# Layer 1 of a four-layer image network: the deformable convolution gathers centered depthwise channels first and multiplies afterwards

## The chip, the cores and the metric

The kernel runs on one core of a Trainium2 chip. A core has five engines that work side by side: TensorE (PE) multiplies matrices, VectorE (DVE) and ScalarE (ACT) work on tiles of 128 partitions, GpSimd (POOL) and SyncE (SP) here mostly start transfers. Sixteen DMA engines move data between the chip's DRAM and the on-chip memory (SBUF). Matrix products land in PSUM, which has eight banks of 128 partitions by 512 f32 values. The metric is the device time of one execution in microseconds (us); lower is better. All arithmetic is f32.

## The reference

The network has four layers on 2 images of 512 channels and 32 x 32 pixels (1024 pixels). Layer 0 is an attention with sampled keys and an MLP, layer 2 a linear attention, layer 3 a normal attention with 8 heads. The change is in layer 1:

```python
x1 = x[:, :256]
x2 = x[:, 256:]
d = conv3x3_depthwise(x1, dw_w, dw_b)          # 256 channels
d = conv1x1(d, pw_w, pw_b)                     # 256 -> 512 channels
mu = d.mean(axis=(2, 3)); var = d.var(axis=(2, 3))
d = (d - mu) / sqrt(var + EPS)                 # per image and channel
off = conv3x3(d, off_w, off_b)                 # 512 -> 18 = 9 taps x (dy, dx)
samples = sum over 4 corners of d[corner] * weight[corner]   # per tap and pixel
dc = einsum('bckhw,ock->bohw', samples, dc_w) + dc_b         # 9 taps, 512 -> 512
dc = layernorm_over_channels(dc) * ln_g + ln_b
das = d * sigmoid(dc)
g = sigmoid(dsc2(max of x2) + dsc2(mean of x2))
x = x * das + x * g
```

A corner outside the image counts as zero. Each tap of each pixel has its own position, read from `off`, so the four corners are gathered by an index.

## The kernel before

The two images are worked one after the other. TensorE's instructions are in an order written by hand: the phases are Python generators, each `yield` is a place where another phase may put its own instructions, and `layers()` (L275) pulls the generators in turn with the helpers `some` and `weave`. The order of the other engines follows from a planner that knows what depends on what. So, if an instruction on TensorE waits, all that stands behind it on TensorE waits too. Memory is given out from pools that open and close like a stack on a left and a right side; a tile that takes memory which another pool has left waits until the last access to it is over.

Layer 1 of image 0 lies beside the MLP of image 1 (`mlp.run(1)`, 32 steps of 8 matmuls). `FOUND` (L449) says how many steps of the features are taken at each MLP step, and from step `MADE` (L450) on two steps of products are taken at each. The phases of layer 1:

- `Features.features` (L1084 on): the depthwise convolution on VectorE (nine operations of 128x1024 for each half of the channels, L1125 and L1129), the channel gate g, the pointwise matmuls (L1145), statistics on VectorE, and the normalised d (L1163).
- `Features.offsets`: d is copied into a tile with a border of zeros, the offset convolution takes 9 taps x 4 channel groups x 4 strips of pixels = 144 matmul instructions for each image (L1186), VectorE adds the bias, and `samples` (L1244) turns positions into indices and the weights of the four corners.
- `Products` (L1293): products first, samples afterwards. For each tap k, d times the tap's 512x512 weights is made for all pixels, in 8 chunks of 128 pixels with 4 matmuls each (L1324). ScalarE copies each result (L1332) and SP writes it to a table in DRAM (L1333), one table of 1024 x 512 for each image and tap. The tap's 1 MB of weights is loaded one tap ahead into one of two buffers.
- `Samples` (L1340): for each tap and chunk two indirect DMAs by POOL (L1376), one for each row of corners, fetch two neighbouring pixels of 512 channels for each of 128 partitions, 512 KB each. VectorE multiplies each corner by its weight and adds it to `dfacc` (L1387): 4 operations of 128x512 for each tap and chunk. `due` lets a tap's gathers begin when its table is whole.
- `gate_image` (L1397): layernorm of `dfacc`, transposes back to channels by pixels, sigmoid, and the new x.

`Linear` (L1450) is layer 2, `Attention` (L1652) layer 3. Its query and key weights `w_q`, `w_k` are loaded at L380, early in the stretch; its weights for the values come later. The products of image 1 are woven with the last samples of image 0, the gate of image 0 and layer 2 of image 0. The queries and keys of layer 3 for image 0 lie beside the last samples of image 1, the values beside layer 2 of image 1 (`BESIDE`, L454). Layer 3 proper starts behind that.

The loop in which the samples are weighed, and the product:

```python
for s in range(4):
    self.net.nc.vector.scalar_tensor_tensor(
        acc, g[:, s, :], self.f.wts[:, c, k, s : s + 1],
        self.f.bias if (k, s) == (0, 0) else acc, ALU.mult, ALU.add)
```

Of the kernel before, what the change touches and what calls it, by code (L numbers as in the profile page):

```python
# [106 lines left out]
def layouts(i):  # L107
# [43 lines left out]
    for h in range(2):  # L151
# [21 lines left out]
        "pw_w": _rows(np.asarray(i["L1_conv_pw_w"]).reshape(C, 256).T),  # L173
        "a_pw_w": _rows(np.asarray(i["L1_conv_a_pw_w"]).reshape(C, 256).T),
# [100 lines left out]
def layers(net, out):  # L275
# [12 lines left out]
    with ExitStack() as later:  # L288
# [41 lines left out]
        with room, ExitStack() as l0b:  # L330
# [20 lines left out]
            products = Products(net, image0, dram, side="right")  # L351
            own0 = ExitStack()
            f0 = Features(net, 0, own0, side="right")
            with ExitStack() as ctx:
                banks["turn"] = net.psum(ctx, "ft_ps", 2), "turn"
                found = f0.run(turn, False)
                made = products.run(f0, turn)
                taken = None
                for i, _ in enumerate(mlp.run(1)):
                    some(found, FOUND[i] if i < len(FOUND) else 0)  # L360
                    if i == len(FOUND):
                        some(found, 99)
                        sums0 = Samples(net, f0, products, own0, 3, side="right")
                        taken = sums0.run()
                    if i >= MADE:
                        for _ in range(2):
                            next(made)

                            if taken is not None and i < 30:
                                sums0.due(taken)  # L370
        with ExitStack() as l1:

            ps_m = net.psum(l1, "l1_m", 5)
            kv_bank = net.bank(l1, "l2_kv")
            banks["turn"] = net.psum(l1, "l1_y", 2), "turn"

            def bank(name):
                return ps_m.tile([128, 512], F32, name=name, tag="bank")

            att = Attention(net, later)  # L380
            l2 = ExitStack()
            linear = Linear(net, l2)
            own1 = ExitStack()
            f1 = Features(net, 1, own1)
            more = net.pool(own1, "df_more", 1)
            sums0.pools += [more]
            found = f1.run(bank, True)
            for i, _ in enumerate(made):
                if i > 1:
                    some(found, 2)  # L390
                if i % 4 < 3:
                    sums0.due(taken)
            some(found, 99)
            sums1 = Samples(net, f1, products, own1, 1)
            sums1.pools += [more]
            tmp = net.pool(own1, "df_tmp", 1)
            made = products.run(f1, turn)
            taken1 = sums1.run()
            aside, ctx2 = None, None
            for i, _ in enumerate(made):  # L400
                if aside is None:
                    if next(taken, None) is None:
                        aside = gate_image(net, f0, sums0, tmp, bank)
                        wait = i + 4
                    continue
                sums1.due(taken1)
                if ctx2 is None and i >= wait:
                    if next(aside) != "gated" and next(aside) != "gated":
                        continue
                    own0.close()  # L410
                    ctx2 = ExitStack()
                    linear.open(ctx2, side="right")
                    extra = net.pool(own1, "df_extra", 4)
                    sums1.pools += [extra] * 4
                    aside = chain(
                        linear.run(0, bank, kv_bank),
                        group_norm_terms(net, linear.tmp, 0, bank),
                    )
                elif ctx2 is not None and i % 3 < 2:
                    next(aside, None)  # L420
            for _ in aside:
                next(taken1, None)
            ctx2.close()
            image0.close()

            att.open_first(later, side="right")
            for _ in att.normalize(0):
                next(taken1, None)
            keys = chain(*(att.queries_keys(0, hp, turn) for hp in range(CC)))
            for i in range(48):  # L430
                next(keys)
                if i % 2 == 0:
                    next(taken1, None)
            some(taken1, 99)
            weave(keys, gate_image(net, f1, sums1, tmp, bank))
            own1.close()
            with ExitStack() as ctx:
                att.open_values(later, side="right")
                linear.open(ctx)
                values = att.values(0, turn)  # L440
                for i, _ in enumerate(linear.run(1, bank, kv_bank)):
                    some(values, BESIDE[i])
            l2.close()
# [5 lines left out]
FOUND = (1, 0, 0, 1, 2, 2, 2, 2, 0, 1, 1, 0, 3, 3, 3)  # L449
MADE = 11  # L450
# [633 lines left out]
class Features:  # L1084
# [4 lines left out]
    def __init__(self, net, b, ctx, **kw):  # L1089
# [4 lines left out]
        self.idx = small.tile([128, 2, 8, 9], mybir.dt.int32, name="idx", tag="idx")  # L1094
        self.wts = small.tile([128, 8, 9, 4], F32, name="wts", tag="wts")
        self.bias = net.load_row("dc_b_row", small)

    def run(self, bank, spread):


        with ExitStack() as ctx:
            yield from self.features(ctx, bank, spread)
        with ExitStack() as ctx:
            yield from self.offsets(ctx, bank, spread)

    def features(self, ctx, bank, spread):
# [3 lines left out]
        self.pw_w, self.a_pw_w = net.load("pw_w", w), net.load("a_pw_w", w)  # L1110
        x_pad = w.tile([128, 34, 34], F32, name="x_pad", tag="x_pad")
        nc.gpsimd.memset(x_pad, 0.0)  # L1112


        dw = tmp.tile([128, 2, 32, 32], F32, name="dw", tag="dw")
        for cc in range(2):
            nc.scalar.copy(
                x_pad[:, 1:33, 1:33], x[:, b, cc, :].rearrange("p (y x) -> p y x", x=32)
            )
            acc = dw[:, cc, :, :]  # L1120
            for t in range(9):
                ky, kx = divmod(t, 3)
                view = x_pad[:, ky : ky + 32, kx : kx + 32]
# [10 lines left out]
        yield  # L1134
        self.channel_gate(bank)
# [3 lines left out]
        flat = dw.rearrange("p c y x -> p c (y x)")  # L1139
        for oc in range(CC):  # L1140
# [15 lines left out]
            mv = tmp.tile([128, 2], F32, name="mv", tag="mv", bufs=2)  # L1156
            nc.vector.bn_aggr(mv, stats)
            rstd = tmp.tile([128, 1], F32, name="rstd", tag="rstd", bufs=2)
            nc.vector.tensor_scalar(rstd, mv[:, 1:2], 1e-5, None, ALU.add)
            nc.scalar.activation(rstd, rstd, AF.Sqrt)  # L1160
            nc.vector.reciprocal(rstd, rstd)
            part = d[:, oc, :]
            nc.vector.tensor_scalar(part, part, mv[:, 0:1], rstd, ALU.subtract, ALU.mult)  # L1163
        yield

    def offsets(self, ctx, bank, spread):
# [4 lines left out]
        d_pad = w.tile([128, CC, 34, 34], F32, name="d_pad", tag="d_pad")  # L1171
        nc.gpsimd.memset(d_pad, 0.0)
        for cc in range(CC):
            nc.scalar.copy(
                d_pad[:, cc, 1:33, 1:33], self.d[:, cc, :].rearrange("p (y x) -> p y x", x=32)
            )
        for _ in range(9 if spread else 1):
            yield


        po = bank("po")
        for t in range(9):
            ky, kx = divmod(t, 3)
            for cc in range(CC):
                for n in range(4):
                    nc.tensor.matmul(  # L1186
                        po[32 * n : 32 * n + 18, :256].rearrange("p (y x) -> p y x", x=32),
                        lhsT=self.off_w[:, cc, t, :],
                        rhs=d_pad[:, cc, 8 * n + ky : 8 * n + ky + 8, kx : kx + 32],
                        start=(t == 0 and cc == 0),  # L1190
                        stop=(t == 8 and cc == CC - 1),
                        skip_group_check=True,
                    )
            yield
# [7 lines left out]
        self.samples(pos, bank)  # L1202

# [40 lines left out]
    def samples(self, pos, bank):  # L1244
# [11 lines left out]
        def new(name, dtype=F32, tag=None):  # L1256
# [14 lines left out]
        row = tmp.tile([128, 8, 9], F32, name="row", tag="row")  # L1271
        nc.vector.scalar_tensor_tensor(
            row, first[:, :, :, 0], 32.0, first[:, :, :, 1], ALU.mult, ALU.add
        )
        for dy in range(2):
            nc.vector.tensor_scalar(self.idx[:, dy], row, 32.0 * dy, None, ALU.add)
# [9 lines left out]
        for k in range(4):  # L1286
            dy, dx = divmod(k, 2)
            nc.vector.tensor_tensor(
                wts[:, :, :, k], near[dy][:, :, :, 0], near[dx][:, :, :, 1], ALU.mult
            )  # L1290


class Products:  # L1293
# [4 lines left out]
    def __init__(self, net, ctx, dram, **kw):  # L1298
        self.net = net
        self.wt = net.pool(ctx, "df_w", 2, **kw)  # L1300
        self.out = net.pool(ctx, "df_y", 4, **kw)
        self.tables = {}
        for b in range(B):
            for k in range(9):
                self.tables[b, k] = dram.tile([HW, C], F32, name="table", tag=f"table{b}_{k}")
        self.made = {(b, k): 0 for b in range(B) for k in range(9)}

    def weights(self, k):
        t = self.wt.tile([128, CC, C], F32, name="dc_w_t", tag="dc_w")
# [669 lines left out]
```

## Time and profile before

| | us |
|---|---|
| median of 3 runs (3950.36 to 3961.6) | 3961.13 |
| the profiled execution, its time | 3949.34 |
| its span, first to last instruction | 3947.6 |
| MLP of image 1 begins | 2420.9 |
| first logits of layer 3 (L1803) | 3406.6 |

The profile is that of one execution. A row of a group of instructions has the line in the program, the engine, the operation, output and inputs, the shape, the count; then busy time in us and the mean of one in ns; then the idle time of the engine ahead of these instructions, and what ended it. In the row of a DMA the last number is the median time in us from issue to landing. A row of a stretch has its length, then for each engine its busy time and the number of its records, the granted clock of TensorE as a share of full speed, the share of the time in which a DMA engine was busy, and GB/s. The rows of the largest groups in the rest of the program are, for comparison:

```profile
L835 PE MATMUL ph<-h,w_t 128*32 128x512 f32 x16384 | 1799.0, 593 | 14.0 <-ACT lo L845 6.4
L1059 PE MATMUL ph<-xn,room 128*128 128x512 f32 x512 | 229.6, 592 | 0.0
L1855 PE MATMUL pt<-cst_t,e 128*128 128x128 f32 x1024 | 148.9, 278 | 6.3 <-ACT aT L1866 3.6
```

### The profile page before, as it was taken

The page shows a single profiled execution, that of the slowest core. Times are in us where ns is not written, and L with a number is a line of the kernel's source. Part 1 is how long each engine was busy: PE and PEld are TensorE (multiplying, and loading weights), DVE is VectorE, ACT ScalarE, POOL GpSimd, SP SyncE. Part 2 cuts the span into 40 slices and gives each one's busy share as a digit, 9 for nine tenths or more (in the row PEclk, how much of TensorE's full clock was granted, in tenths as well). Part 3 has the DMA queues.
Part 4 walks back from the last instruction along what each step waited for, and adds up shares of the span by engine and source line. Part 5 has one row for each costly group of instructions (what it writes and reads, how often), then busy time and mean ns, then how long its engine had stood idle before and what let it go on. Part 6 is the DMA issues. An engine that isn't in the chain of part 4 may idle for free.

```text
span 3947.6 us, 60251 instructions
## 1 busy us (share of the span) xinstructions
PE 3837.4 (97%) x25580; PEld 1516.4 (38%) x25580; DVE 2951.5 (75%) x3312; ACT 2539.7 (64%) x2866; POOL 347.9 (9%) x324
## 2 busy tenths in 40 slices
PE   7999999999999999999998999999898999999999
PEld 4432232222322222222333444444343444455555
DVE  6999999999999999999995114043576887566565
ACT  7999999999999999999994211211121212245544
POOL 0000000000000000000000000032363553000000
PEclk9999999999999999999998999999999999999999
DMA  3000000000000000000011000065677996000000
GB/s 108 1 23 22 23 23 1 22 23 23 12 12 23 23 22 1 23 23 22 1 54 54 0 0 24 21 209 194 254 284 274 346 357 224 1 5 8 1 19 25
DMA packets 90482, 274.82 MB, mean 70 GB/s; under 512 B 9141, under 2 KB 10677, under 8 KB 86885
## 3 DMA queue, kind: packets, MB, share of 16 engines
q0 software_dynamic: 42432, 154.39, 10.7%
q1 hardware_dynamic: 47780, 116.58, 8.2%
q8 instruction: 202, 3.31, 0.3%
q14 instruction: 68, 0.55, 0.0%
HBM read 228.72 MB, written 42.21 MB: 69 GB/s over the span
## 4 chain that ended last, share of the span: by engine, by line
PE 76%; ACT 10%; DVE 6%; DMA 4%; issue 2%; POOL 1%; SPq 0%; POOLq 0%; ACTq 0%; DVEq 0%
PE ph L835 36%; PE py L1324 6%; PE ph L1059 5%; PE acc L1048 5%; PE sim L856 4%; ACT h L824 3%; PE pl L1803 3%; DVE dfacc L1387 3%; DMA got<-table,idx 3%; PE pq L1736 3%; PE po L1818 3%; PE pt L1855 3%; ACT hi L847 2%; ACT lo L845 2%; ACT ab L480 2%
## 5 line engine op out<-in xcount | busy, mean ns | idle before, releaser
L835 PE MATMUL ph<-h,w_t 128*32 128x512 f32 x16384 | 1799.0, 593 | 14.0 <-ACT lo L845 6.4
L815 DVE TENSOR_TENSOR h<-ab 128x1024 f32<-128x1024 f32 x1024 | 1205.4, 1218 | 74.6 <-PE ph L835 73.5
L835 PEld LDWEIGHTS ph<-h,w_t 128*32 128x32 f32 x16384 | 547.5, 110 | 1238.2 <-issue 1066.3
L824 ACT ACTIVATE h<-h 128x1024 f32<-128x1024 f32 x832 | 870.4, 1066 | 41.3 <-DVE h L815 40.4
L848 DVE SCALAR_TENSOR_TENSOR hi<-lo,low_w,hi 128x1024 f32<-128x1024 f32 x512 | 654.4, 1278 | 27.6 <-ACT hi L847 27.0
L847 ACT ACTIVATE hi<-ph,size_b,size 128x1024 f32<-128x1024 f32 x512 | 620.4, 1212 | 16.3 <-PE ph L835 10.5
L845 ACT ACTIVATE lo<-ph,vec_t 128x1024 f32<-128x1024 f32 x512 | 571.1, 1115 | 5.0 <-PE ph L835 5.0
L1387 DVE SCALAR_TENSOR_TENSOR dfacc<-got,wts,dfacc 128x512 f32<-128x512 f32 x560 | 402.3, 746 | 197.9 <-DMA got<-table,idx 190.4
L1324 PE MATMUL py<-dc_w_t,d 128*128 128x512 f32 x1152 | 519.4, 606 | 24.8 <-ACT y L1332 24.8
L1332 ACT COPY y<-py 128x512 f32<-128x512 f32 x144 | 83.3, 584 | 474.1 <-PE py L1324 442.1
L1376 POOL DMA_INDIRECT got<-table,idx x288 | 328.0, 1139 | 459.1 <-DVE dfacc L1387 152.4
L1324 PEld LDWEIGHTS py<-dc_w_t,d 128*128 128x128 f32 x1152 | 220.1, 194 | 303.0 <-issue 266.6
L1901 ACT ACTIVATE e<-pl,m 128x1024 f32<-128x1024 f32 x128 | 143.5, 1121 | 224.5 <-DVE m L1893 224.5
L1893 DVE TENSOR_REDUCE m<-pl 128x1 f32<-128x1024 f32 x128 | 150.7, 1219 | 145.0 <-PE pl L1803 145.0
L856 PE MATMUL sim<-hi,w 128*32 128x512 f32 x2048 | 246.8, 592 | 0.6 <-DVE hi L848 0.6
L1059 PE MATMUL ph<-xn,room 128*128 128x512 f32 x512 | 229.6, 592 | 0.0
L1048 PE MATMUL acc<-h,mlp_w_t 128*128 128x512 f32 x512 | 229.2, 592 | 0.0
L1067 ACT ACTIVATE h<-ph,vec_t 128x512 f32<-128x512 f32 x64 | 44.0, 687 | 247.6 <-PE ph L1059 247.5
L1112 POOL MEMSET x_pad<- 128x1156 f32 x2 | 2.1, 1068 | 2086.8 <-PE pb L959 2086.8
L1855 PE MATMUL pt<-cst_t,e 128*128 128x128 f32 x1024 | 148.9, 278 | 6.3 <-ACT aT L1866 3.6
L1855 PEld LDWEIGHTS pt<-cst_t,e 128*128 128x128 f32 x1024 | 118.6, 142 | 93.7 <-issue 61.7
L1048 PEld LDWEIGHTS acc<-h,mlp_w_t 128*128 128x128 f32 x512 | 97.3, 190 | 122.4 <-issue 122.4
(232 smaller groups left out, 2457.1 us busy)
## 6 DMA issues: line engine op xcount, KB each, us to landing
table<-y SPq DMA_DIRECT2D x144, 256.0 KB, 5.6
ab<-feat_d SPq DMA_DIRECT2D x64, 512.0 KB, 4.3
dc_w_t<-in_dc_w_dram SPq DMA_DIRECT2D x18, 1024.0 KB, 6.1
got<-table,idx POOLq DMA_INDIRECT x288, 7.0
room<-in_mlp_w_dram SPq DMA_DIRECT2D x1, 4096.0 KB, 15.6
mlp_w_t<-in_mlp_w_dram SPq DMA_DIRECT2D x1, 4096.0 KB, 12.0
w_qkv_t<-in_w_qkv_dram SPq DMA_DIRECT2D x3, 1024.0 KB, 5.3
out_dram<-x_all SPq DMA_DIRECT2D x12, 256.0 KB, 2.0
```

Of the source, the lines that this page charges most:

```text
L815: nc.vector.tensor_tensor(h1.rearrange("p (y x) -> p y x", x=32), at_x[:, k : k + 1, :].to_broadcast([128, 32, 32]), at_y[:, k, :].unsquee ...
L824: nc.scalar.activation(h1, h1, AF.Relu)
L835: nc.tensor.matmul(ph[32 * t : 32 * t + 32, half(n)], lhsT=w2[:, c0 : c0 + 32], rhs=pair[t // 2][:, half(n)], start=True, stop=True, skip_ ...
L845: nc.scalar.activation(lo, phs[0], AF.Relu, bias=b2_lo)
L847: nc.scalar.activation(hi, phs[1], AF.Relu, bias=size_b, scale=size)
L848: nc.vector.scalar_tensor_tensor(hi, lo, low_w, hi, ALU.mult, ALU.add)
L856: nc.tensor.matmul(sim[32 * t : 32 * t + 32, half(n)], lhsT=w3[:, 30 - j : 62 - j], rhs=sums[t][:, half(n)], start=(j == 0), stop=(j == 30 ...
L1048: nc.tensor.matmul(accs[oc], lhsT=self.w2[:, m, 128 * oc : 128 * oc + 128], rhs=hs[m], start=(m == 0), stop=(m == 15),)
L1059: nc.tensor.matmul(ph, lhsT=self.w1[:, k, 128 * m : 128 * m + 128], rhs=xn[:, k, :], start=(k == 0), stop=(k == CC - 1),)
L1324: nc.tensor.matmul(py, lhsT=f.d[:, cc, 128 * c : 128 * c + 128], rhs=w[:, cc, :], start=(cc == 0), stop=(cc == CC - 1),)
L1387: self.net.nc.vector.scalar_tensor_tensor(acc, g[:, s, :], self.f.wts[:, c, k, s : s + 1], self.f.bias if (k, s) == (0, 0) else acc, ALU.mult,
L1855: nc.tensor.transpose(pt[:, 128 * c : 128 * c + 128], e[:, 128 * k : 128 * k + 128], ident)
```

## The change

Samples and products change places. The pointwise convolution is linear, and its output is normalised per channel, so d is the pointwise weights, scaled by 1/std, times the depthwise channels less their mean over the image; the biases drop out. The sum over corners can then be made on the 256 depthwise channels, and the pointwise weights can be multiplied into the weights of the offset and of the deformable convolution beforehand.

- The depthwise output is centered on VectorE and copied into the bordered tile `pad`. d itself is still made by the pointwise matmuls, for the gate; its normalisation and the channel gate move to the end of `offsets`.
- TensorE transposes the centered channels (16 transposes for each image), and four DMAs by SP write one table for each image: 1024 pixels x (the pixel, the pixel one row below) x 256 channels, 2 MB. One gather of two neighbouring pixels brings all four corners, 512 KB: 72 gathers for each image instead of 144.
- The offset weights are folded with the scaled pointwise weights `pw_n` (8 matmuls of 162 columns), and the offset convolution has 72 instructions for each image instead of 144. The offset weights' tile is now in a pool that opens when the pools of `features` have closed.
- `Folded`: for each tap and half of the channels 4 matmuls make the folded weights, 72 matmuls for each image. Image 0 loads each tap's weights into the tile `out_w` of layer 0, one buffer; image 1 has two.
- `Deform`: VectorE sums the corners of two samples (a pair; 36 pairs for each image), TensorE transposes the sum (4), ScalarE copies it, and TensorE multiplies it by the folded weights (4 matmuls of 512 columns), accumulating over the nine taps in one PSUM bank. Chunks are now the outer loop, taps the inner. VectorE adds the bias when a chunk is done.
- 18 pairs of image 0 lie in the MLP stage, the other 18 beside the features of image 1; the gate of image 0 lies beside the rest of those features; the fold of image 1 beside layer 2 of image 0; then come the 36 pairs of image 1. The query and key weights of layer 3 are loaded in the middle of these, and layer 2's weights are loaded once more for image 1.

```diff
+            two = turned[:, 2 * q : 2 * q + 2, :]
+            nc.scalar.copy(two, pt.rearrange("p (u i) -> p u i", i=256))
...
+        nc.sync.dma_start(out=rows[:, :, 0, :], in_=turned)
+        nc.sync.dma_start(out=rows[:96, :, 1, :], in_=turned[32:, :, :])
+        nc.sync.dma_start(out=rows[96:, :7, 1, :], in_=turned[:32, 1:, :])
+        nc.sync.dma_start(out=rows[96:, 7, 1, :], in_=turned[96:, 7, :])
+
+    def offsets(self, ctx, bank, held):
         net, nc, b = self.net, self.net.nc, self.b
         w = net.pool(ctx, f"ft_offw{b}")
         tmp = self.tmp = net.pool(ctx, f"ft_off{b}")
         self.off_w, self.taps = net.load("off_w", w), net.load("taps", w)
...
+        off_w = w.tile([128, 2, 9, 18], F32, name="off_f", tag="off_f")
+        pw = bank("pw").rearrange("p (i m) -> p i m", m=256)[:, :, : 9 * 18]
+        for i in range(2):
+            for cc in range(CC):
+                nc.tensor.matmul(
+                    pw[:, i, :],
+                    lhsT=self.pw[:, cc, 128 * i : 128 * i + 128],
+                    rhs=self.off_w[:, cc, :, :].rearrange("p t o -> p (t o)"),
...
+class Folded:
...
+        nxt = load(0)
         for k in range(9):
...
+            w, nxt = nxt, None
+            if ahead and k < 8:
+                nxt = load(k + 1)
+            for i in range(2):
+                pw = bank("pw")
                 for cc in range(CC):
                     nc.tensor.matmul(
+                        pw,
+                        lhsT=f.pw[:, cc, 128 * i : 128 * i + 128],
                         rhs=w[:, cc, :],
                         start=(cc == 0),
                         stop=(cc == CC - 1),
                     )
+                nc.scalar.copy(self.w[k][:, i, :], pw)
+                if i == 1 and nxt is None and k < 8:
+                    nxt = load(k + 1)
                 yield
...
+class Deform:
...
+    def run(self, turn, po, flush=()):
...
+        for j in range(self.PAIRS):
+            if self.pending is not None:
+                self.product()
+            pool, t = self.sums.popleft()
+            pt = self.turn("pt")
+            for q in range(4):
+                nc.tensor.transpose(
+                    pt[:, 128 * q : 128 * q + 128],
+                    t[:, q // 2, 128 * (q % 2) : 128 * (q % 2) + 128],
+                    self.net.cst("ident"),
+                )
+            tpool, turned = self.new("turned", [128, 512])
+            nc.scalar.copy(turned, pt)
+            self.free["sum"].append(pool)
+            self.sum()
+            self.pending = j, tpool, turned
...
+    def product(self):
...
+            for i in range(2):
+                at = 128 * (2 * q + i)
+                nc.tensor.matmul(
+                    self.out,
+                    lhsT=turned[:, at : at + 128],
+                    rhs=self.folded.w[k][:, i, :],
+                    start=(k == 0 and i == 0),
+                    stop=(k == 8 and i == 1),
+                )
```

In `gate_image` the accumulator comes as two tiles of four chunks instead of one tile of eight. The stage tables become:

```diff
-FOUND = (1, 0, 0, 1, 2, 2, 2, 2, 0, 1, 1, 0, 3, 3, 3)
-MADE = 11
+FOUND = (1, 0, 0, 0, 2, 3, 3, 3, 3, 2, 1, 1, 1)
+FIRST = 18
+
+BOTH = (2,) * 9 + (1, 0, 0, 0, 0, 2, 2, 2, 2, 1)
```

## The prediction, made before the changed kernel had run

> **What bounds the kernel now.** I read the slices first, then the stretch that the change touches in the view of windows, then the chain of waits in it, then single instructions.
>
> ```profile
> PE 3837.4 (97%) x25580; PEld 1516.4 (38%) x25580; DVE 2951.5 (75%) x3312; ACT 2539.7 (64%) x2866; POOL 347.9 (9%) x324
> PEclk9999999999999999999998999999999999999999
> ```
>
> TensorE is busy for 97% of the span, and its clock is near full except in the slices from 22 to 32. The changed code lies between 2420.9 us (the second image's MLP begins) and 3406.6 us (the first logits of layer 3). What lies before and after is the same code, so the sum is made for these 985.7 us alone.
>
> ```profile
> core 0: us, PE busy (x) PEld busy (x) DVE busy (x) ACT busy (x) POOL busy (x), PEclk, DMA share, GB/s
> 2804.50:3005.00 200.50, 176.22 (x657) 77.93 (x656) 136.63 (x210) 35.19 (x61) 101.24 (x76) 0.95 0.75 276
> 3071.00:3223.00 152.00, 151.54 (x472) 74.03 (x471) 131.59 (x199) 32.71 (x54) 84.59 (x80) 1.00 0.93 353
> 3223.00:3254.00 31.00, 23.32 (x55) 10.54 (x54) 25.76 (x44) 5.37 (x9) 16.34 (x15) 0.89 0.92 347
> 2420.90:3406.60 985.70, 936.83 (x2914) 429.00 (x2913) 562.54 (x885) 188.49 (x296) 339.47 (x296) 0.98 0.60 219
> ```
>
> PE is busy for 936.8 of 985.7 us. From 2804.5 on it waits, its clock drops to 0.95 and 0.89, and DMA is busy up to 93%. So: TensorE's work is the bound, with the samples' gathers close behind it in the middle. The costliest rows of the stretch say what both are made of:
>
> ```profile
> L1387 DVE SCALAR_TENSOR_TENSOR dfacc<-got,wts,dfacc 128x512 f32<-128x512 f32 x560 | 402.3, 746 | 197.9 <-DMA got<-table,idx 190.4
> L1324 PE MATMUL py<-dc_w_t,d 128*128 128x512 f32 x1152 | 519.4, 606 | 24.8 <-ACT y L1332 24.8
> L1376 POOL DMA_INDIRECT got<-table,idx x288 | 328.0, 1139 | 459.1 <-DVE dfacc L1387 152.4
> table<-y SPq DMA_DIRECT2D x144, 256.0 KB, 5.6
> dc_w_t<-in_dc_w_dram SPq DMA_DIRECT2D x18, 1024.0 KB, 6.1
> got<-table,idx POOLq DMA_INDIRECT x288, 7.0
> ```
>
> A matmul overlaps its successor, so its 606 ns isn't its price. The chain of waits and the timeline give the price:
>
> ```profile
> 2592.98 6.87 PE acc L1048 x16
> 3128.33 0.60 PE L1522 MATMUL pk<-cst_t,qkf 128*128 128x128 f32 x4
> 3128.97 0.58 ACT L1524 COPY kf<-pk 128x512 f32<-128x512 f32 x1 [0.29 <-PE pk L1522]
> 3251.65 10.85 PE L1324 MATMUL py<-dc_w_t,d 128*128 128x512 f32 x18
> 3604.07 0.60 PE L1855 MATMUL pt<-cst_t,e 128*128 128x128 f32 x4
> 3604.51 1.02 PE L1736 MATMUL pq<-h,w_qkv_t 128*128 128x512 f32 x2
> ```
>
> An f32 matmul of 512 columns has two records, so 16 records in 6.87 us are 8 instructions at **0.86 us**. Four transposes take 3604.51 - 3604.07 = 0.44 us. An ACT copy of a bank starts 0.04 us after its transposes end and takes 0.58.
>
> **TensorE's work before and after.** Removed: 9 taps x 8 chunks x 4 x 2 images = 576 product matmuls, 494.2 us. Removed too: half of the offset convolution's 288 instructions (L1186, 0.11 us each by their spacing), 15.9 us. Added: the fold, 9 x 2 x 4 x 2 = 144 matmuls, 123.6; 72 pairs of 4 transposes and 4 product matmuls, 0.44 + 3.43 = 3.87 each, 278.6; 32 transposes of the depthwise channels, 3.5; 16 matmuls of 162 columns that fold the offset weights, 4.3 at 0.86 x 162/512 each. Unchanged in the stretch: MLP 219.7, pointwise 27.5, linear layer 57.4, attention's queries, keys and values 71.2, small ones 12.5. With the offsets and the products, before is 914.4 us and after **814.3**: 100 us less work. Elapsed before is 985.7, so 71 us are idle or slow clock. The question is how much idle the new order has. I go through it stage by stage; dependencies are read from the code.
>
> **MLP with image 0 (works 379.3 us).** Now 18 pairs are done in this stage. (1) load of the offset weights: its memory is that of the depthwise tiles, so it waits for the four table writes, and TensorE's fold of them stands straight behind the last transposes, with the whole MLP behind it. ACT's last copy ~1, table 7 to 11, load 2.6 to 5.1 (324 KB: by the 256 KB row of 2.0 us for an output, scaled, and by its own row before, 5.1): 12 to 17 us idle, 2 to 5 us of slow clock after it: 18. (2) load of each of the 9 weight tiles of 1 MB into one buffer (it was double): issued when the last fold matmuls that read the old tile are done; a step of MLP (8 matmuls, 6.87 us) covers the row's 6.1: 0, and if MLP weren't there some 5 us a tap. (3) the products of pair j follow its transposes directly where no MLP lies between (10 of 18): 0.04 + 0.58 + 0.06 + 0.17 for latency, a bubble of 0.85: 8.5. (4) change-over 2. Sum 408.
>
> The table is 2 MB in four writes with pieces of 1 KB. No row shows this write. The nearest is 256 KB in 2.0 us (out_dram, uncontended) or 5.6 (beside gathers). At the 353 GB/s of the window above it takes 6 us and a start-up of 1 to 2: ends 7 and 11. The Trainium skill, "DMA: Bandwidth & Descriptors", section "Anatomy of one DMA", fits about 2.0 us plus bytes over 436 GB/s: 6.8 us for all of it, an estimate. I take 9, near the row that carries gathers beside it; by the rule each image would gain 2 us.
>
> **18 pairs with image 1's features (works ~95).** DVE sums the four corners of two samples in 6 scalar_tensor_tensor and 2 tensor_scalar of 128x256. Neither is in the trace at that size. Its rows are 746 ns at 512 and 1277 at 1024 columns (tensor_scalar 542 and 808), so on that slope 0.48 and 0.41 us; by spacing (0.66 us at 512) about 0.40 and 0.33. A pair thus takes 3.0 to 3.7 us; I take 3.0, by the spacing, since these operations stand back to back. The 3x3 depthwise steps (1.2 us each, two a pair) lie on DVE beside 9 pairs: 5.4 a pair against TensorE's 4.7. Sum 108.
>
> **Gap before image 1's fold (works 17).** Sum of the chain: last transposes, copies and gate's sigmoids on ACT 6, table 9, offset weights 4, fold and offset convolution 12, positions and samples on DVE among the first image's gate operations 12; after those SP may issue 1.5 MB of layer 2 weights and the first 1 MB tap, beside 3 MB of first gathers: ~14. That is 57 us, 40 of them idle; with a cold start 59.5. Before, product matmuls lay over all of this.
>
> **Fold and layer 2 of image 0 (works 90.5):** 94.5. **36 pairs of image 1:** 3.87 + 0.85 = 4.72 each: 170. DVE (3.0), POOL (2 gathers, 1.33 apart: 2.7) and DMA (1 MB in 4.7 us, 223 GB/s) are below it. Attention's q and k weights are now loaded here; SP's queue is empty, nothing waits. **Rest to 3406.6:** 107 (before 114.7, from 3291.9), as the normalised input waits 2.5 us for the last product instead of 7.4 for samples.
>
> At the bubbles a rule speaks against this change. "TensorE: Matmul & The Clock Gate", section "A second HAM failure mode: psum-queue depth-cycling", says that short idle times between groups of matmuls, bank after bank, can make the clock go back and forth. The row: the single wait of 7.4 us ahead of 3251.65 put 18 records at 0.60 us for 0.43, 3.1 us lost. No row has 0.85 us of idle time in every 4.7. Ends: 0, or half of the time at half clock, 36 x 3.87 x 0.5 = 70 us. I take 0: in the windows of this trace with up to 4% short gaps the clock stays at 0.99 to 1.00, and 0.89 comes only with gaps of 7 us. By the rule the whole gain would be gone.
>
> **Sum.** 408 + 108 + 59.5 + 94.5 + 170 + 107 = 947, against 985.7: **39 us less**. Idle rises from 71 to 133 as 100 us of work goes. The profiled run has a span of 3947.6 and a time of 3949.3, so 3910. The median of the runs shown, 3961.1, lies 11.8 above that run; half of it added gives **3916**.
>
> **Rivals.**
> *Covers better than I count.* TensorE's order lets the planner move ACT and DVE work of the gate out of the chain; the gap costs 15 idle us for 40, the first load 8 for 18, DVE 0 for 13, a bubble of 0.5: 25 + 10 + 13 + 13 = 61 us more: 3855. For it: each stall was added up in series. Against: the order on TensorE is fixed. Chance 0.2.
> *Nothing gained.* The change does away with TensorE work but its stall is only moved: if the chain to image 1's fold is 95 us instead of 57, 3950. For it: gate operations of DVE stand in the chain. Chance 0.09.
> *Slower: the gathers' return sets the pair.* Each pair needs two gathers of 512 KB. Six buffers hold about three pairs; a buffer is held for its landing and 1.5 us of sums. At the row's median of 7.0 us six buffers give a pair per 2.8 us and are covered. The longest landing in this trace is 19.8 us: 7.1 a pair. Each us above 4.7 costs 54 us over the 54 pairs after the MLP, so it decides from 5.4 a pair (landing 14.7 us); at 16 us, 5.8 a pair: +60, 3976. For it: DVE waited 190 us for gathers before. Against: bytes per sample are halved, and no table writes of 256 KB lie beside them. The oscillating clock ends at the same place. Chance 0.09.
>
> **Numbers.** My own case 0.62: 3880 to 3945. The range 3868 to 3958 takes in the nearer part of the first rival and of "nothing gained". A difference under 0.3% (12 us) can't be told from none. Faster 0.82, same 0.09, slower 0.09.
>
> **What would show it.** Pairs of image 1 at 4.7 us with 0.85 between transposes and products, and a granted clock of 0.97 or more there; one idle time of 12 to 17 us ahead of the offset weights' fold (L1236) near 2500 (nine MLP steps and the pointwise matmuls after 2420.9); about 40 us of idle TensorE ahead of the second fold. Wrong if pairs take over 5.4 us with DVE waiting for gathers, if the clock in the pairs is under 0.9, or if either idle time is twice or half of that.

## The result, and the profile after

The changed kernel takes 3928.08 us (median of 4 runs, 3923.71 to 3930.33), against 3960.43 us for the kernel before in the same comparison: a ratio of 0.9923, with a 95% interval of 0.9904 to 0.9941. The profiled execution has a span of 3924.5 us, 23 less than before; the medians differ by 32, since the profiled run of the kernel before (3949.34) lay below its four timed runs. The page of the changed kernel begins as follows (busy time and share of each engine, then the granted clock in 40 slices), and further down has these groups and transfers:

```profile
PE 3749.9 (96%) x25356; PEld 1492.9 (38%) x25356; DVE 2798.6 (71%) x3348; ACT 2524.4 (64%) x2837; POOL 173.2 (4%) x180
PEclk9999999999999999999998999999998999999999
...
L1507 PE MATMUL po<-fold,turned 128*128 128x512 f32 x576 | 270.8, 611 | 60.8 <-ACT turned L1483 40.6
L1454 DVE SCALAR_TENSOR_TENSOR sum<-got,wts,sum 128x256 f32<-128x256 f32 x432 | 183.9, 479 | 2.6
L1432 POOL DMA_INDIRECT got<-table,idx x144 | 159.1, 1105 | 584.5 <-DVE sum L1454 418.2
...
got<-table,idx POOLq DMA_INDIRECT x144, 4.9
```

TensorE is busy for 87 us less, yet the span falls by 23: most of the work that was saved came back as idle time. POOL is idle until VectorE frees a buffer (418 us) and a gather lands in 4.9 us instead of 7.0, so over the whole program gathers wait for VectorE. TensorE's waits for ScalarE's copy, 40.6 us, are new.

The view of windows shows where the idle time lies. The rows are the stages of the prediction's sum: MLP with image 0; 18 pairs with image 1's features; the gap; fold and layer 2; the 36 pairs; the rest up to layer 3's first logits at 3381.0. (In the trace the fold's last matmuls lie at the start of the fifth row: the pairs run from 3092.2 to 3272.8.)

```profile
core 0: us, PE busy (x) PEld busy (x) DVE busy (x) ACT busy (x) POOL busy (x), PEclk, DMA share, GB/s
2419.50:2829.30 409.80, 386.46 (x1105) 177.60 (x1104) 125.34 (x267) 66.75 (x102) 41.03 (x44) 0.98 0.26 84
2829.30:2946.50 117.20, 91.78 (x250) 42.20 (x249) 92.30 (x196) 20.86 (x34) 51.22 (x31) 0.93 0.46 146
2946.50:2997.80 51.30, 21.99 (x234) 16.12 (x232) 24.51 (x53) 13.85 (x22) 6.49 (x8) 0.69 0.39 138
2997.80:3088.00 90.20, 90.20 (x299) 45.23 (x300) 34.57 (x61) 15.43 (x26) 5.67 (x6) 0.97 0.42 151
3088.00:3272.80 184.80, 156.37 (x463) 73.34 (x461) 118.23 (x312) 27.98 (x46) 59.17 (x61) 1.00 0.58 188
3272.80:3381.00 108.20, 104.77 (x348) 52.04 (x348) 33.82 (x55) 27.74 (x37) 0.73 (x2) 1.00 0.05 19
```

| stage, us | forecast | measured |
|---|---|---|
| MLP with image 0 | 408 | 409.8 |
| 18 pairs with image 1's features | 108 | 117.2 |
| gap | 59.5 | 51.3 |
| fold of image 1, layer 2 of image 0 | 94.5 | 94.4 |
| 36 pairs of image 1 | 170 | 180.6 |
| rest | 107 | 108.2 |
| sum | 947 | 961.5 |

The timeline of TensorE has the waits that matter. First the one in the MLP stage, then one beside image 1's features, then two in the gap, then a pair of image 1 and the end of a chunk:

```profile
2489.08 1.04 PE L1210 MATMUL pt<-cst_t,dw 128*128 128x128 f32 x8
2502.49 4.66 PE L1236 MATMUL pw<-off_w_t,pw_n_t 128*128 128x162 f32 x16 [12.38 <-DMA off_w_t<-in_off_w_dram]
...
2868.19 3.78 PE L1507 MATMUL po<-fold,turned 128*128 128x512 f32 x4 [11.98 <-DVE dfacc L1515]
...
2963.04 4.66 PE L1236 MATMUL pw<-off_w_t,pw_n_t 128*128 128x162 f32 x16 [11.55 <-DMA off_w_t<-in_off_w_dram]
2997.79 6.36 PE L1388 MATMUL pw<-dc_w_t,pw_n_t 128*128 128x512 f32 x8 [15.16 <-DMA dc_w_t<-in_dc_w_dram]
...
3153.40 3.70 PE L1507 MATMUL po<-fold,turned 128*128 128x512 f32 x8 [0.73 <-ACT turned L1483]
3158.27 1.98 PE L1507 MATMUL po<-fold,turned 128*128 128x512 f32 x4 [0.73 <-ACT turned L1483]
3161.22 1.98 PE L1507 MATMUL po<-fold,turned 128*128 128x512 f32 x4 [0.97 <-DVE dfacc L1515]
```

From 3153.40 to 3158.27 is one pair: 4.87 us. Between 3158.27 and 3161.22 the product of one chunk's last tap ends, VectorE adds the bias and thereby empties the only output bank, and TensorE waits 0.97 us for it, as chunks have an odd number of taps and half of them end inside a pair. The same wait is 11.98 us at 2868.19. What VectorE did up to there is in the row of that part of the stage, and in one line of VectorE's timeline:

```profile
2829.30:2868.20 38.90, 21.02 (x58) 9.42 (x56) 32.26 (x60) 4.93 (x7) 27.35 (x12) 0.85 0.46 149
2839.68 0.35 DVE L1452 TENSOR_SCALAR sum<-got,wts 128x256 f32<-128x256 f32 x1 [6.32 <-DMA got<-table,idx]
```

VectorE is busy for 32.3 of these 38.9 us and waits 6.3 us for a gather. From 2839.68 on it works without a pause, and the bias stands in its queue behind sums and depthwise steps.

### The profile page after: what moved, and what is told of

Same layout as the page of the kernel before. It is cut to its first block, busy times and chain, and to the rows that moved or that the text cites. A ratio compares the mean times of both kernels' runs of the same rounds, so it can differ in the third digit from the quotient of the medians.

```text
span 3924.5 us, 59277 instructions
## 1 busy us (share of the span) xinstructions
PE 3749.9 (96%) x25356; PEld 1492.9 (38%) x25356; DVE 2798.6 (71%) x3348; ACT 2524.4 (64%) x2837; POOL 173.2 (4%) x180
## 4 chain that ended last, share of the span: by engine, by line
PE 82%; ACT 11%; DVE 4%; issue 1%; DMA 1%; SPq 0%; ACTq 0%; DVEq 0%
PE ph L854 36%; PE po L1507 6%; PE acc L1067 6%; PE ph L1078 6%; PE sim L875 4%; PE pw L1388 3%; ACT h L843 3%; PE pl L1928 3%; PE po L1943 3%; PE pq L1861 3%; PE pt L1980 3%; ACT hi L866 2%; ACT lo L864 2%; ACT ab L499 2%; PE po L1018 1%
## 5 line engine op out<-in xcount | busy, mean ns | idle before, releaser
L1507 PE MATMUL po<-fold,turned 128*128 128x512 f32 x576 | 270.8, 611 | 60.8 <-ACT turned L1483 40.6
L1483 ACT COPY turned<-pt 128x512 f32<-128x512 f32 x72 | 42.2, 586 | 309.3 <-PE pt L1477 305.0
L1452 DVE TENSOR_SCALAR sum<-got,wts 128x256 f32<-128x256 f32 x144 | 48.1, 365 | 239.2 <-PE pt L1477 211.0
L1454 DVE SCALAR_TENSOR_TENSOR sum<-got,wts,sum 128x256 f32<-128x256 f32 x432 | 183.9, 479 | 2.6
L1432 POOL DMA_INDIRECT got<-table,idx x144 | 159.1, 1105 | 584.5 <-DVE sum L1454 418.2
L1507 PEld LDWEIGHTS po<-fold,turned 128*128 128x128 f32 x576 | 105.0, 192 | 188.3 <-issue 108.5
L1980 PEld LDWEIGHTS pt<-cst_t,e 128*128 128x128 f32 x1024 | 118.6, 142 | 93.7 <-issue 61.4
## 6 DMA issues: line engine op xcount, KB each, us to landing
mlp_w_t<-in_mlp_w_dram SPq DMA_DIRECT2D x1, 4096.0 KB, 13.3
```

Of the source, the lines that this page charges most:

```text
L1454: nc.vector.scalar_tensor_tensor(t[:, q, :], g[:, s, :], w, t[:, q, :], ALU.mult, ALU.add)
L1507: nc.tensor.matmul(self.out, lhsT=turned[:, at : at + 128], rhs=self.folded.w[k][:, i, :], start=(k == 0 and i == 0), stop=(k == 8 and i = ...
L1980: nc.tensor.transpose(pt[:, 128 * c : 128 * c + 128], e[:, 128 * k : 128 * k + 128], ident)
```

## The experiments

Ten kernels were run, each compared with the kernel before. Gains below are against the changed kernel, by the span of the profiled execution (3924.5). The profiled executions reach the MLP of image 1 between 2418.4 and 2421.6 us, ahead of all that the edits touch, so a gain by the span is good to some 3 us; smaller ones are read from the stages.

| kernel | median, us | ratio to before, 95% interval | span, us |
|---|---|---|---|
| new order of transposes and products | 3915.51 | 0.9901, 0.9884 to 0.9918 | 3913.0 |
| two output banks | 3922.65 | 0.9922, 0.9906 to 0.9939 | 3919.9 |
| offset weights early | 3910.69 | 0.9888, 0.9872 to 0.9905 | 3908.7 |
| half gathers | 3925.09 | 0.9924, 0.9908 to 0.9941 | 3923.1 |
| new order and two banks | 3893.48 | 0.9832, 0.9796 to 0.9869 | 3892.2 |
| first tap early | 3913.65 | 0.9885, 0.9849 to 0.9921 | 3911.2 |
| all four | 3868.01 | 0.9767, 0.9732 to 0.9803 | 3867.8 |
| all four and more | 3864.42 | 0.9759, 0.9723 to 0.9795 | 3862.3 |
| two corners summed | 3867.03 | 0.9773, 0.9753 to 0.9793 | 3864.3 |
| first corner on ScalarE | 3851.67 | 0.9735, 0.9715 to 0.9755 | 3848.3 |

### The order of transposes and products

```diff
         for j in range(self.PAIRS):
-            if self.pending is not None:
+            late = bool(self.free["turned"])
+            if self.pending is not None and not late:
                 self.product()
...
             self.sum()
+            if self.pending is not None:
+                self.product()
             self.pending = j, tpool, turned
```

> Transposes of pair j+1 stand ahead of the products of pair j on TensorE wherever two buffers for the turned sum exist (after the MLP stage); nothing else changes. My theory (the bubble behind ScalarE's copy sets the pair, TensorE's work is the bound): the 0.89 us between transposes and products goes, a pair of image 1 takes 4.0 us instead of 4.87, 36 x 0.89 = 32 us there and up to 8 beside image 1's features, less some 4 us at the ends of chunks where VectorE's bias now waits in the open: 30 to 38 us faster than the changed kernel, span near 3890. Rival (gathers or VectorE's sums set the pair): the pair stays above 4.6 us, gain under 10 us.

Measured: 11.5 us faster. Neither theory got the sum right: the pair fell as forecast, the gain did not follow. The timeline of TensorE in this kernel shows a chunk's end and the pair after it:

```profile
3162.13 1.88 PE L1510 MATMUL po<-fold,turned 128*128 128x512 f32 x4
3165.98 1.98 PE L1510 MATMUL po<-fold,turned 128*128 128x512 f32 x4 [1.96 <-DVE dfacc L1518]
3167.80 0.60 PE L1478 MATMUL pt<-cst_t,sum 128*128 128x128 f32 x4
3168.24 3.60 PE L1510 MATMUL po<-fold,turned 128*128 128x512 f32 x8
3171.67 0.60 PE L1478 MATMUL pt<-cst_t,sum 128*128 128x128 f32 x4
3172.11 3.60 PE L1510 MATMUL po<-fold,turned 128*128 128x512 f32 x8
```

A pair now takes 3172.11 - 3168.24 = 3.87 us, TensorE's bare work, so neither gathers nor sums set the pair. But the wait for the bias has grown from 0.97 to 1.96 us, and a wait of 4.2 us for the group norm terms appears that the slower pairs had covered. The 36 pairs take 164.4 us, 16 less and not 32. Beside image 1's features, where up to 8 us more were expected, 7 were lost: that stage has 124.5 us instead of 117.2, with two waits of 7.8 and 6.8 us for the bias.

### Two output banks

```diff
+            outs = []
...
+            def po_two(name):
+                outs.append(name)
+                return (po_bank, held)[len(outs) % 2](name)
...
-            deform0.turn, deform0.po = turn, po_bank
+            deform0.turn, deform0.po = turn, po_two
...
-            for i, _ in enumerate(deform1.run(turn, po_bank)):
+            for i, _ in enumerate(deform1.run(turn, po_two)):
```

> The accumulated output alternates between two PSUM banks from image 1's features on (the second is the bank of the offset convolution, which is idle then). My theory (the next chunk's first product waits for VectorE's bias on the one bank): the single wait of 12 us ahead of 2868 and the six waits of 0.97 to 1.25 us at the ends of chunks go, 12 + 6 = 18 us, of which VectorE's own backlog beside the features gives back up to half: 9 to 18 us faster than the changed kernel. Rival (the 12 us are VectorE's backlog alone): the wait moves to the transposes that wait for sums, gain 4 to 7 us from the ends of chunks alone.

Measured: 4.6 us faster, the size that the rival forecast, but near what two executions differ by (the ratio to the kernel before, 0.9922, is that of the changed kernel). The stages tell more. The 36 pairs take 175.4 us instead of 180.6: the waits at the ends of chunks are gone. The 12 us at 2868 are gone too, but the stage has 118.8 us, no less than 117.2. TensorE's timeline in this kernel shows what took their place:

```profile
2859.71 0.69 PE L1483 MATMUL pt<-cst_t,sum 128*128 128x128 f32 x2 [3.60 <-DVE sum L1460]
2879.24 0.44 PE L1483 MATMUL pt<-cst_t,sum 128*128 128x128 f32 x2 [1.40 <-DVE sum L1460]
2899.78 1.09 PE L1483 MATMUL pt<-cst_t,sum 128*128 128x128 f32 x4 [5.09 <-DVE sum L1460]
```

The waits are for VectorE all the same, now for its sums. Ahead of the first two VectorE had worked without a pause for 9 us or more, so there it was behind. The third has another cause. GpSimd took 14.31 us to issue one gather, where it commonly takes 0.94, and VectorE then waited for the gathers behind it:

```profile
2877.47 14.31 POOL L1438 DMA_INDIRECT got<-table,idx  x1 [2.73 <-DVE sum L1460]
2895.11 0.50 DVE L1458 TENSOR_SCALAR sum<-got,wts 128x256 f32<-128x256 f32 x1 [3.54 <-DMA got<-table,idx]
2897.31 0.35 DVE L1458 TENSOR_SCALAR sum<-got,wts 128x256 f32<-128x256 f32 x1 [1.70 <-DMA got<-table,idx]
```

So the bound of this stage is VectorE together with the gathers that it waits for: 12.9 us of such waits in this kernel, 6.3 in the changed one.

### Both together

> Both edits together: transposes of pair j+1 ahead of the products of pair j, and two PSUM banks for the output in turn. My theory now (in the 36 pairs of image 1 TensorE is the bound once both waits are gone; beside image 1's features VectorE is): the 36 pairs take 36 x 3.87 = 139 us and up to 8 of waits, against 181 in the changed kernel, and the stretch from the end of the MLP to the end of image 1's pointwise matmuls shrinks from 117 us by no more than 10: 34 to 46 us faster than the changed kernel. Rival (the two edits only share one gain): 11 + 5 = 16 us.

Measured: 32.3 us faster, just under the 34 to 46 forecast, and twice the 16 that the edits gave one by one. Windows of this kernel, first the 18 pairs with image 1's features, then the 36 pairs:

```profile
2831.20:2948.00 116.80, 93.52 (x250) 43.36 (x249) 92.56 (x197) 20.30 (x34) 62.88 (x31) 0.91 0.43 147
3091.90:3241.00 149.10, 144.93 (x453) 72.11 (x451) 116.72 (x309) 26.99 (x45) 68.89 (x61) 0.98 0.70 234
```

The 36 pairs fall from 180.6 to 149.1 us and are busy with TensorE's work for 145 of these. Each edit alone had left the other's wait on the path. The first row has not moved: 116.8. VectorE waits 17.7 us for gathers in it.

### VectorE's part: two of four corners

```diff
-                for s in range(4):
+                for s in range(2):
                     w = self.f.wts[:, c, k, s : s + 1]
```

> The kernel with the new order of transposes and two output banks, in which VectorE sums two of the four corners and leaves out the other two (4 of its 8 operations of each pair); gathers and TensorE's work are as before. My theory (beside image 1's features VectorE is the bound, in the 36 pairs of image 1 TensorE is): the stretch from the end of the MLP to image 1's last pointwise matmul falls from 117 us to 95 to 107, the 36 pairs stay at 149 within 4. Rival (that stretch is set by the chain of the features, statistics and pointwise matmuls, not by the sums): it stays within 4 us of 117.

The windows of the same two stages:

```profile
2830.10:2927.10 97.00, 85.33 (x251) 40.28 (x250) 67.49 (x131) 20.42 (x34) 47.44 (x31) 1.00 0.49 171
3070.80:3213.00 142.20, 141.96 (x453) 70.86 (x451) 66.13 (x177) 27.20 (x45) 58.10 (x61) 1.00 0.73 246
```

With 25 us less of VectorE's work the first stage is 20 us shorter, so beside image 1's features VectorE's sums are on the path. They are not there alone: shorter sums also give gather buffers back sooner, GpSimd's longest issue in the stage falls from 14.3 to 8.4 us, and VectorE's waits for gathers fall from 17.7 to 13.7. What of the 20 us came that way is not separated. The 36 pairs go from 149 to 142, 3 us below the lower end: TensorE is busy there all the time, and its one wait with two banks, 3.9 us for group norm terms of VectorE, is gone.

### Half gathers

```diff
-                out=g.rearrange("p s i -> p (s i)"),
+                out=g[:, 0:2, :].rearrange("p s i -> p (s i)"),
...
-                            t[:, q, :], g[:, s, :], w, t[:, q, :], ALU.mult, ALU.add
+                            t[:, q, :], g[:, s % 2, :], w, t[:, q, :], ALU.mult, ALU.add
```

> Each gather brings one pixel and the pixel below it (256 KB instead of 512), and the two right-hand corners take the left-hand values: two of the four corners of each sample are left out. VectorE and TensorE do the same work. My theory (gathers are hidden behind TensorE): pairs of image 1 stay at 4.87 us, the whole within 8 us of the changed kernel (the first gathers after the gap may come 3 to 5 us sooner). Rival (the gathers' return sets the pair): 4.87 falls by 0.5 us or more, 25 us or more in all.

Measured: 1.4 us faster by the span, and a ratio of 0.9924 like that of the changed kernel. Pairs of image 1 stay at 4.87 us, and the wait for the first tap's weights goes from 15.2 to 14.4 us. The rival of the prediction that the gathers' return sets the pair is excluded for these pairs. Beside image 1's features VectorE still waits 6.9 us for gathers, as against 6.3, so their bytes do not set that wait.

### Offset weights early

```diff
             self.pad = w.tile([128, 2, 34, 34], F32, name="pad", tag="pad")
+            if self.b == 0:
+                self.off_w = self.net.load("off_w", w)
+                self.off_f = w.tile([128, 2, 9, 18], F32, name="off_f", tag="off_f")
...
```

> For image 0 alone the offset weights and their folded tile lie in memory that is free from the start, so their load does not wait for the table writes. My theory: the idle time of 12.4 us ahead of the fold of the offset weights in the MLP stage goes, with 1 to 2 us of slow clock behind it: 11 to 14 us faster than the changed kernel. Rival (the stall is moved: the offset convolution or the positions then wait for the table writes): a wait of 6 us or more appears ahead of L1252 or L1326, gain under 6 us.

Measured: 15.8 us faster, above the 11 to 14 expected; the MLP stage falls by 15.4. The wait of 12.4 us is 0.24, and no other takes its place: the table writes and ScalarE's copy into the folded tile lie beside an MLP step.

```profile
2491.30 2.47 PE L1242 MATMUL pw<-off_w_t,pw_n_t 128*128 128x162 f32 x16 [0.24 <-ACT dwt L1219]
```

The 16 matmul records of the fold take 2.47 us instead of 4.66: the granted clock is 1.00 in them, and was 0.50 behind the wait.

### First tap early

```diff
             image0.close()
+            tap0 = ExitStack()
+            pool0 = net.pool(tap0, "df_w0", 1, side="right")
...
+            w0 = load1(0)
             gate = gate_image(net, f0, deform0.acc, tmp, bank)
             weave(gate, found)
+            folded1 = Folded(net, image1)
+            some(folded1.tap(f1, turn, 0, w0), 99)
+            tap0.close()
             own0.close()
...
```

> The first tap's weights for image 1's fold go to memory that is free when image 0's last pair is done, and the first tap is folded ahead of layer 2's first matmuls; the other taps are loaded as before. My theory (TensorE waits 15 us at the second fold because that load waits for memory of image 0 and then shares the DMA engines): 10 to 15 us faster than the changed kernel. Rival (the gap is moved: the second tap, or layer 2's weights, land no sooner): a wait of 6 us or more on one of these behind the first tap, gain under 7 us.

Measured: 13.3 us faster. The fold follows the gate's last transposes at once, and the second tap, loaded behind, is there in time, as the timeline of TensorE shows:

```profile
2984.17 1.09 PE L1578 MATMUL pt<-cst_t,dfacc 128*128 128x128 f32 x4
2985.06 13.02 PE L1414 MATMUL pw<-dc_w_t,pw_n_t 128*128 128x512 f32 x24
2997.92 3.60 PE L1633 MATMUL pqk<-x_all,wqk_t 128*128 128x512 f32 x8
```

### Together, and the fastest version

> All four edits: the order of transposes and products, two output banks, offset weights loaded early for image 0, first tap loaded early for image 1. If each wait is on TensorE's path by itself, the gains add: 34 to 46 for the first two, 16, and 10 to 15: 60 to 77 us faster than the changed kernel, a span of 3848 to 3865. If they cover one another, under 50.

Measured: 56.7 us faster by the span, 60.1 by the medians, at or just under the lower edge. One by one the three parts are 32.3 + 15.8 + 13.3 = 61.4, so the waits stood on TensorE's path nearly independently. The 36 pairs took 152 us here and 149 with the first two edits alone: TensorE has one wait of 7.0 us among them, for VectorE's mean in the group norm terms, where it had 3.9 before; these terms lie elsewhere now that the first tap is folded ahead of layer 2.

> As the kernel with all four edits, with the offset weights loaded early for image 1 too and two more gather buffers instead of three for image 0's second half. The wait of 11 us ahead of image 1's offset fold goes; the positions' memory still waits for the table writes, so I expect 3 to 9 us more than the four edits; nothing more if the first gathers set the fold's end, and a loss of up to 5 if the missing buffer shows.

Measured: 5.5 us more than the four edits by the span, of which 2.7 lie ahead of the MLP of image 1, so about 3 come from the edit. The 11 us wait ahead of image 1's offset fold is gone, but waits for the positions and the channel gate (5.5 us ahead of its matmuls) took nearly all of it back: the gap is 34.9 us instead of 36.0.

The last kernel takes up what the summed corners showed, and gives ScalarE part of VectorE's work:

```diff
-                        nc.vector.tensor_scalar(t[:, q, :], g[:, 0, :], w, None, ALU.mult)
+                        nc.scalar.activation(t[:, q, :], g[:, 0, :], AF.Identity, scale=w)
```

> The fastest kernel so far (four edits, image 1's offset weights early too), with the first corner's product of each sample made by ScalarE instead of VectorE: 2 of VectorE's 8 operations of each pair, about 0.6 us a pair. If VectorE is the bound beside image 1's features: 18 x 0.6 = 11 us at most there, 4 to 11 faster than the kernel before it (3862 span). If ScalarE, which also copies the turned sums, is held up behind gathers, it is slower by up to 10.

Measured: 14.0 us more, over the upper end. Here are the stage beside image 1's features and TensorE's wait among the 36 pairs, first without the edit, then with it:

```profile
2813.50:2931.00 117.50, 95.91 (x250) 43.70 (x249) 93.44 (x202) 20.61 (x34) 56.57 (x33) 0.91 0.46 153
3082.71 0.59 PE L1798 MATMUL pm<-mean,cst_t 128*128 128x4 f32 x2 [7.40 <-DVE mean L1796]
...
2814.90:2924.80 109.90, 90.85 (x249) 42.81 (x248) 83.70 (x168) 35.56 (x68) 48.80 (x33) 0.94 0.50 163
3074.73 0.39 PE L1805 MATMUL pvar<-spread,cst_t 128*128 128x4 f32 x2 [2.09 <-DVE spread L1802]
```

The stage gained 7.6 us, near half of the 14. The 36 pairs gained as much, which the expectation had left out: they fall from 152.4 to 144.8 us, as the wait for VectorE's group norm terms falls from 7.4 to 2.1 us and the granted clock there rises from 0.97 to 1.00. At 3851.67 us it is the fastest kernel of this study, 0.9735 of the kernel before.

## Why the prediction was right, point by point

The direction and the time were right: 3928 measured, 3916 forecast. The stretch shrank by 24 us by the spans where the sum said 39; the 15 us between them have named places. In part it was luck: four stages were over by 22.8 us in all, and a gap that was shorter by 8.2 took a third of that back.

- **TensorE is the bound, and its work falls by 100 us.** Busy time fell by 87 us over the program. The bare pair of 3.87 us is what the new order showed. (Of the slices of the clock before, the row has one below 0.9, the 22nd, and not those from 22 to 32.)
- **Bubble of 0.85 us in each pair.** Right in kind, small in size: from transposes to products there are 1.33 us for 1.29, and from products to the next transposes 3.54 for 3.43. A pair is 4.87 us instead of 4.72, 36 x 0.15 = 5.4 us. That the copy's wait is on the path was shown by turning the order round.
- **A step that failed: nothing at the ends of chunks.** The sum had only transposes and products in a pair; that the next chunk has no bank until VectorE has added the bias was left out. In the 36 pairs that is 4 x 1.3 = 5.2 us, which makes up the rest of the 10.6 that this stage is over.
- **Beside image 1's features: 108 forecast, 117 measured.** VectorE was named as the bound for nine pairs, at 5.4 us each. Two edits that left VectorE's work as it is left the stage at 117 to 119; half the corners made it 97. So VectorE's queue is on the path, and its term was 9 us too small. Two things were missing in it: besides sums and depthwise steps the queue has bias, statistics and centering, and VectorE waits 6.3 us for a gather at the start of the stage. Both stand ahead of the bias for which TensorE waited 12 us. No run takes that wait for a gather away by itself, so how the 9 us divide stays open.
- **Offset weights in the MLP stage: 18 forecast.** Taking the wait away gave 15.8. The wait itself is 12.4 us, and a slow clock follows. The table writes took from 2490.8, the first issue, to 2499.5, when the load that waited for them was issued: 8.7 us, near the 9 that was chosen by the row with gathers beside it; for image 1 it was 8.0. The 6.8 by the fit of the Trainium skill ("DMA: Bandwidth & Descriptors", "Anatomy of one DMA") would have been short by 1 to 2. That fit is given for transfers that GpSimd issues, and SP issued these.
- **The gap: 59.5 forecast, 51.3 measured.** Most links were a little dear: the load of the offset weights took 2.9 us for 4, and the first tap was there 11.2 us after the issue of the loads for 14. TensorE was idle for 29.3 us of it, where about 40 were forecast. The wait for the first tap was on the path, as loading it early showed. The wait of 11.6 us for the offset weights was not so alone: with it gone, and the first tap early, the gap lost only 1.1 us, as other waits stood close behind.
- **The fold, 94.5, and the rest, 107.** 94.4 and 108.2. (By its own terms the rest is 114.7 - 7.4 + 2.5 = 109.8.)
- **The oscillating clock.** The rule of "TensorE: Matmul & The Clock Gate" that was weighed does not describe these pairs: with 0.73 us of idle time in each 4.87 the granted clock is 1.00 from 3088 to 3272.8. The end taken, 0, holds. The page tells the rule of a bf16 kernel; these products are f32. (In the row that it was weighed by, the wait is 7.68 us, ahead of 3251.20; the 7.4 stand ahead of 3296.)
- **Gathers.** Half the bytes changed nothing that can be told, and the pairs of image 1 do not wait for them. The landing of 19.8 us that this rival was sized by was no slow return: of these, 15.4 us were the issue on GpSimd, as the last section shows. Beside image 1's features gathers do count, by 6.3 us.
- **Covers better than counted, and nothing gained.** Neither came: every stall that was added up was there, some of them shorter, and the chain of the gap took 51 us, not 95.

## What to carry to other kernels

When work is cut from the engine that is the bound, look at what the removed work had covered: of 87 us of saved TensorE time 64 came back as idle time, much of it behind loads, copies and sums that the old products had lain over. In a loop of transpose, copy and product the next transposes belong ahead of the products, and every bank that another engine empties at the end of an accumulation needs a second one; either edit alone leaves the other's wait on the path, so try them together. A load that waits for memory of a tile still being written out is a wait on two transfers in series; give it memory of its own where a few kilobytes can be found, and look whether another wait stands close behind (of image 1's 11 us only 1 was gained). Where VectorE works without a pause, look also at how long GpSimd takes to issue each gather.

## What the runs showed of the hardware

Short waits can slow TensorE's clock too. In the kernel with the new order the products behind a wait for the bias mostly kept full speed, but not always:

```profile
3203.77 1.98 PE L1510 MATMUL po<-fold,turned 128*128 128x512 f32 x4 [2.00 <-DVE dfacc L1518]
3243.59 3.67 PE L1510 MATMUL po<-fold,turned 128*128 128x512 f32 x4 [2.38 <-DVE dfacc L1518]
```

Four records took 1.98 us behind 2.00 us of idle time, at a granted clock of 1.00, and 3.67 behind 2.38, at 0.50. In the same kernel a wait of 1.97 us at 2922.44 was followed by four in 3.50. So waits of about 2 us were sometimes followed by half speed, and those of up to 1.25 us in the changed kernel's 36 pairs never were.

GpSimd can take long to issue a gather while VectorE works. Here is one issue of the kernel before, then one of the changed kernel with the next behind it:

```profile
2859.24 15.41 POOL L1376 DMA_INDIRECT got<-table,idx  x1 [0.81 <-DVE dfacc L1387]
...
2850.06 16.31 POOL L1432 DMA_INDIRECT got<-table,idx  x1 [2.17 <-DVE sum L1454]
2866.67 0.94 POOL L1432 DMA_INDIRECT got<-table,idx  x1 [0.30 <-issue]
```

The median of the changed kernel's 144 issues is 0.94 us. In all twelve kernels, every issue of over 5 us lies beside a stretch of VectorE without a pause of over 0.1 us, and is over at most 0.9 us after that stretch. So the two go together; that VectorE's work is the cause was not tested. The gather of the first line landed 19.8 us after its issue began, the longest of that trace.
